# An LSTM cell issued by halves of its units, with the weight sums of a fast product made sooner and in even shares

## The chip, the cores and the metric

The kernel runs on one core of a Trainium2 chip. The metric is device time in microseconds (us) of one execution. A core has TensorE (PE; its weight loads are listed as PEld), VectorE (DVE), ScalarE (ACT), GpSimd (POOL) and SyncE (SP), which run their own instruction streams and wait for one another through semaphores. Here SP only issues DMA transfers, and ACT issues some as well.

## The reference

An LSTM with a residual connection, in fp32. The batch is 32, there are T = 512 steps, and the inputs and the state have 512 elements.

```python
a = x[:, t] @ Wx + b + h @ Wh          # 32 x 2048: gates i, f, o, g
i, f, o = sigmoid(a[:, :512]), sigmoid(a[:, 512:1024]), sigmoid(a[:, 1024:1536])
g = tanh(a[:, 1536:])
c = f * c + i * g                      # c starts at 0, h at cond_1024
h = o * tanh(c)
out[:, t] = x[:, t] + h
```

The product h @ Wh depends on the step before. The product x @ Wx does not, and can be computed ahead.

## The kernel before

**Layout.** The 2048 gate columns of a step are held as a bank of 128 partitions by 512 columns: partition = column group j (four of them) times 32 batch rows, and the 512 columns are two halves of the units, each of which holds i, f, o, g of 64 units. PE works in four column groups of 32, one for each j, so that four matmuls with 32 columns of stationary data run side by side. The profile records each fp32 matmul as two instructions.

**One step.** h_part(t) (L211) adds h @ Wh into the bank: 16 matmuls, for k = 0 to 3 and in each for j = 0 to 3; the stationary operand is the transposed h, `state["ht"][:, k]`. k = 0 and 1 come from the first half of the units, k = 2 and 3 from the second. cell(t) then runs on ACT and DVE: sigmoid of i and f (L225), tanh of g (L226), sigmoid of o (L227) on ACT; f·c for both halves at once (L228), i·g for each half (L230), their sum for each half (L232) on DVE; tanh of c on ACT for each half (L234); h = o·tanh(c) for each half (L236), and two transposes in blocks of 32x32 (L242) on DVE that give the next ht. POOL adds the residual (L247) and SP stores it. From step SPLIT = 478 on, a bank pair is used and the whole cell runs once for each half.

**The products ahead.** The first HEAD = 24 steps use plain products: plain_block (L159), 32 matmuls for each step. Those of steps 0 to 4 go to banks of their own before the first h_part. Those of steps 5 to 23 are emitted two to a step between the h_parts of the head, into one of three banks; keep() (L718) adds the bias on DVE into a parking place in SBUF, and SP stores that into DRAM (kept, L719) and loads it back (L571) when its step is near. Then come 20 groups of 24 steps, whose x @ Wx is made by a scheme with fewer multiplications: each group has 20 slots with seven products of four matmuls (L480, the stream). Its left operands are sums of x (ubuf, made by DVE at L391; the pair sums at L438 and on belong to a loaded group), its right operands are sums of Wx (vdram in DRAM, loaded row by row into vring at L559). The products are evacuated by ACT and DVE (L526 to L542) into cbuf, summed there by DVE (L356), stored to DRAM and loaded into xw some steps later. About 23.3 such matmuls are emitted between two h_parts. Before h_part(t+1) ACT copies xw into the gate bank (seed_step, L588), from step 5 on.

**The weight sums.** tail_sums are eight DVE operations on the loaded Wx; v_slot(s), for 20 slots, makes up to three sums of three DVE operations (L630), which go into vring and ubuf while these are not yet in use, and queues a store of two or three DMAs. flush_v, called after the cell, issues the queued stores from ACT (L642).

**The order of the work** is written out by hand: each engine runs what is emitted for it in program order. In the head each step does, in order: h_part; SP's stores and loads; then for each chunk of PE work the matmuls, and behind the first chunk's matmuls the cell and flush_v, and then keep; then DVE jobs (tail sums, v_slots, four pair sums, early_seeds) from one list, as long as an allowance of 3000 ns of estimated cost for that plain block is left (a v_slot counts 2100); last the seed copy for the next step. When five jobs or fewer are left, the first rows of vring are loaded (load_v_ahead), and when none is left the second group is loaded.

Of the kernel before, what the change touches and what calls it, by code (L numbers as in the profile page):

```python
# [7 lines left out]
F32 = mybir.dt.float32  # L8
AF = mybir.ActivationFunctionType
# [3 lines left out]
P = 128  # L13
B = 32
T = 512
# [4 lines left out]
H = P // 2  # L20
# [3 lines left out]
HEAD = 24  # L24
# [6 lines left out]
KEPT = 5  # L31
# [38 lines left out]
def cost_dve(cols):  # L70
    return 150 + 1.05 * cols
# [17 lines left out]
def kernel(  # L89
# [10 lines left out]
    nc = tc.nc  # L100
    add, sub = nc.vector.tensor_add, nc.vector.tensor_sub
# [34 lines left out]
    def load_x(c, a=0, b=TC):  # L136
        nc.sync.dma_start(
            out=xnat[:, xslot(c), a:b].rearrange("p t q b -> p (t q b)"), in_=x[c][:, a * P : b * P]
        )
# [33 lines left out]
    state = {}  # L173
    sring = [work.tile([P, 2, 4, H], F32, name=f"s_{i}") for i in range(2)]
    oring = [work.tile([P, 2, H], F32, name=f"o_{i}") for i in range(1)]
    fc = work.tile([P, 2, H], F32, name="fc")
    ig = work.tile([P, 2, H], F32, name="ig")
    tanh_c = work.tile([P, P], F32, name="tanh_c")
    hbuf = work.tile([P, P], F32, name="hbuf")
    htr = [work.tile([P, NJ, B], F32, name=f"ht_{i}") for i in range(2)]  # L180
# [34 lines left out]
    def cell(t):  # L215
        n, tt = divmod(t, TC)
        s, nxt = sring[t % 2], sring[(t + 1) % 2]
        o = oring[0]
        ht = htr[t % 2]
        by_gate = lambda a: a.rearrange("p (h g u) -> p h g u", g=G, u=H)  # L220
        for part in [(0,), (1,)] if is_split(t) else [(0, 1)]:
            i = slice(part[0], part[-1] + 1)
            units = slice(H * part[0], H * (part[-1] + 1))
            g = by_gate(half_of(t, part[0])) if is_split(t) else by_gate(bank_of(t))
            nc.scalar.activation(s[:, i, 0:2], g[:, :, 0:2], AF.Sigmoid)  # L225
            nc.scalar.activation(s[:, i, 2], g[:, :, 3], AF.Tanh)  # L226
            nc.scalar.activation(o[:, i], g[:, :, 2], AF.Sigmoid)  # L227
            nc.vector.tensor_mul(fc[:, i], s[:, i, 1], s[:, i, 3])  # L228
            for u in part:
                nc.vector.tensor_mul(ig[:, u], s[:, u, 0], s[:, u, 2])  # L230
            for u in part:
                add(nxt[:, u, 3], fc[:, u], ig[:, u])  # L232
            for u in part:
                nc.scalar.activation(tanh_c[:, HALVES[u]], nxt[:, u, 3], AF.Tanh)  # L234
            for u in part:
                nc.vector.tensor_mul(hbuf[:, HALVES[u]], o[:, u], tanh_c[:, HALVES[u]])  # L236
            if t == T - 1:
                add(tanh_c[:, units], hbuf[:, units], x_last[:, units])
                nc.sync.dma_start(out=out[n][:, tt * P + units.start : tt * P + units.stop], in_=tanh_c[:, units])
                continue  # L240
            for u in part:
                nc.vector.transpose(ht[:, 2 * u : 2 * u + 2].rearrange("p q b -> p (q b)"), hbuf[:, HALVES[u]])  # L242
        if t == T - 1:
            return
        state["ht"] = ht
        oc = ocr[t // 2 % 2]
        (nc.gpsimd if t < T - 8 else nc.vector).tensor_add(oc[:, tt % 2], x_of(t), ht)  # L247
        if tt % 2 == 1 or t == T - 2:
            m = tt % 2 + 1
            stores.append(  # L250
                lambda: nc.sync.dma_start(
                    out=out[n][:, (tt + 1 - m) * P : (tt + 1) * P],
                    in_=oc[:, 0:m].rearrange("p t q b -> p (t q b)"),
                )
            )
            if t == T - 2:
                stores.pop()()
# [7 lines left out]
    room = {"dve": 0.0}  # L265
# [171 lines left out]
    def load_group(g):  # L437
        nc.sync.dma_start(  # L438
            out=xs[g % 2][:, :, 0:4],
            in_=xg[g].rearrange("p (k s m) -> p k s m", k=6, s=4),  # L440
        )
# [249 lines left out]
    def load_seeds(pairs, queue):  # L691
        for i, j in pairs:
            queue.dma_start(out=seeds[i], in_=bias[j : j + 1].to_broadcast([P, W]))
# [14 lines left out]

    parks = [cbuf[:, 8 + i // 2, i % 2 * 2 : i % 2 * 2 + 2].rearrange("p s c -> p (s c)") for i in range(4)]
    park_banks = [xbank[1], xbank[2], bbank]
    kept_stores = []

    def keep(p):
        n = p - KEPT
        dst = parks[n % 4]
        add(dst, park_banks[n % 3], bias_full)  # L718
        kept_stores.append(lambda: nc.sync.dma_start(out=kept[n], in_=dst))  # L719

    with tc.manual_schedule():
# [18 lines left out]
            )  # L740
        load_x(0, 5, 8)
        load_x(1)
        load_x(2)
        load_seeds(((4, 3), (5, 1)), nc.sync)
        load_group(0)
        for n in range(3):
            for j in range(NJ):
                nc.tensor.matmul(
# [6 lines left out]
        for c in range(4):  # L755
            for t in range(KEPT):
                plain_block(t, c, bank_of(t))
        dve_jobs = []
        dve_jobs += [(cost_dve(1024), f) for f in tail_sums(0, 4)]
        for t in range(KEPT):  # L760
            add(bank_of(t), bank_of(t), bias_full)
        dve_jobs += [(cost_dve(1024), f) for f in tail_sums(4, 8)]
        for s in range(R):
            dve_jobs.append((2100.0, lambda s=s: v_slot(s)))
        dve_jobs += [(cost_dve(768), lambda i=i: pair_sum(0, i)) for i in range(4)]
        dve_jobs.append((1600.0, early_seeds))

        fill = [("plain", p) for p in range(KEPT, HEAD)]
        HEAD_STEPS = STREAM0
# [13 lines left out]
        for t in range(T):  # L783
# [8 lines left out]
                load_x(c)  # L792
            if t == SPLIT - 4:
                load_x(NCHUNK - 1)
            if t + 3 >= KEPT and t + 3 < HEAD + NG * GS and t >= 2:
                if t == 2:
                    pass
                load_xw(t + 3)

            if t < HEAD_STEPS:  # L800
                target = head_work * (t + 1) / HEAD_STEPS
                chunks = []
                while done_work < target - 200 and n_plain < HEAD - KEPT:
                    chunks.append(("plain", KEPT + n_plain))
                    n_plain += 1
                    done_work += PLAIN
                n = int((target - done_work) / PROD * 4 + 0.5) if n_plain == HEAD - KEPT else 0
                if t == HEAD_STEPS - 1 and n:
                    n = R * 7 * 4 - pos[0]
                left = n  # L810
                while left > 0:
                    m = min(left, 24)
                    chunks.append(("stream", m))
                    left -= m
                done_work += n * PROD / 4
                for i, (kind, m) in enumerate(chunks):
                    if kind == "plain":
                        bank = park_banks[(m - KEPT) % 3]
                        room["dve"] = 3000.0
                        for cc in range(4):  # L820
                            plain_block(m, cc, bank)
                        if i == 0:
                            cell(t)
                            flush_v()
                        keep(m)
                        if m == HEAD - 1:
                            plains_done = t
                        while dve_jobs and room["dve"] > 0:
                            cost, f = dve_jobs.pop(0)
                            f()  # L830
                            room["dve"] -= cost
                    else:
                        load_v_ahead()
                        u_ahead(m)
                        room["dve"] = m * PROD / 4 * 1.5
                        evacuate()
                        if late_seeds_due and plains_done < t - 1:
                            late_seeds_due.pop()()
                        if t >= HEAD_STEPS - 3 and dve_jobs:
                            dve_jobs.pop(0)[1]()  # L840
                        u_ahead(m + 24)
                        while wqueue and room["dve"] > 0:
                            w_op()
                        seed_banks(m)
                        emit_matmuls(m)
                        if i == 0:
                            cell(t)
                            flush_v()
                            if t == plains_done + 1:
                                load_seeds(((0, 0), (1, 1), (2, 2)), nc.scalar)  # L850
                if t + 1 >= KEPT:
                    seed_step(t + 1)
                if len(dve_jobs) <= 5 and not v_stores:
                    load_v_ahead()
                if group_loaded == 1 and n_plain == HEAD - KEPT and not dve_jobs:
                    assert not v_stores
                    load_group(1)
                    group_loaded = 2
                    dve_jobs += [(cost_dve(768), lambda i=i: pair_sum(1, i)) for i in range(4)]
                continue  # L860


# [91 lines left out]
```

## Time and profile before

| | |
|---|---|
| median of 3 runs | 3188.89 us (3188.05 to 3189.84) |
| the profiled execution | 3188.77 us |
| its span, first to last instruction | 3186.9 us |
| mean granted TensorE clock | 0.996 |
| busy PE, DVE, ACT, POOL | 3140.8, 2161.1, 1344.6, 233.3 us |
| first recurrent product ends | 30.96 us |
| head: recurrent products of steps 4, 5, 6 and 10 end | 72.39, 91.37, 108.04, 152.27 us |
| 24 steps of the steady part | 144.84 to 145.44 us |

The page of a profile gives the busy time of each engine, groups of instructions by line with the idle time ahead of them and what ended it, and the DMA queues. Other views show the waits of a window, the timeline, and the busy time in chosen stretches with the granted clock. L numbers are lines of the kernel. The same lines stand three higher up in the changed kernel from the end of the cell on (L588 becomes L585, L480 L477), and the cell's own lines move a little.

### The profile page before, as it was taken

The numbers are of one execution on the slowest core, as the hardware profiler recorded it, in microseconds if no ns is written. First come the engines' busy times: TensorE is split into PE (matmuls) and PEld (weight loads), VectorE is DVE, ScalarE is ACT, GpSimd is POOL, SyncE is SP. The second block draws the span as 40 slices with busy tenths as digits, with TensorE's granted clock in tenths as the row PEclk, the third lists the DMA queues.
The fourth block names the chain that finished last, engine by engine and source line by source line (L and its number), as shares of the span: only waits on it lengthen the run. The fifth ranks groups of instructions, "written<-read, shape, count | busy, mean of one in ns | idle before, by whom it ended". The sixth has DMA issues, their size and how long they took to land.

```text
span 3186.9 us, 104607 instructions
## 1 busy us (share of the span) xinstructions
PE 3140.8 (99%) x41944; PEld 2017.6 (63%) x41944; DVE 2161.1 (68%) x6763; ACT 1344.6 (42%) x4525; POOL 233.3 (7%) x508
## 2 busy tenths in 40 slices
PE   9799999999999999999999999999999999999998
PEld 6445666666666666666666666656666666666555
DVE  5477767676676767677666767676776767676644
ACT  0134444444444444444444444444444444444344
POOL 0000000000000000000000000000000000000000
PEclk9999999999999999999999999999999999999999
DMA  8777787777777777777787777777777877777831
GB/s 289 251 266 255 236 263 243 254 242 241 261 243 258 229 251 252 253 247 249 241 255 258 226 262 237 258 241 256 242 246 248 255 258 228 247 246 237 261 96 38
DMA packets 310997, 766.64 MB, mean 241 GB/s; under 512 B 49392, under 2 KB 92144, under 8 KB 310000
## 3 DMA queue, kind: packets, MB, share of 16 engines
q1 hardware_dynamic: 296800, 740.82, 71.7%
q10 hardware_dynamic: 13712, 19.14, 1.7%
q8 instruction: 331, 5.42, 0.7%
q14 instruction: 154, 1.26, 0.1%
HBM read 577.04 MB, written 182.71 MB: 238 GB/s over the span
## 4 chain that ended last, share of the span: by engine, by line
PE 83%; DVE 8%; DMA 4%; ACT 2%; issue 1%; SPq 1%; ACTq 1%; DVEq 0%
PE gbank L211 48%; PE xbank L480 26%; PE bbank L480 5%; DVE cbuf L356 3%; PE xbank L211 2%; PE xbank L159 2%; DVE ubuf L391 1%; DMA xw<-xwd 1%; ACT tanh_c L234 1%; DMA xs<-in_L_cond_Wx_dram 1%; DVE ig L230 1%; ACTq L642 1%; DVE fc L228 1%; DVE cbuf L536 1%; ACT cbuf L535 1%
## 5 line engine op out<-in xcount | busy, mean ns | idle before, releaser
L211 PE MATMUL gbank<-wh_sb,ht 128*32 128x512 f32 (+1 forms) x16288 | 1837.6, 581 | 24.0 <-ACT gbank L588 16.5
L211 PEld LDWEIGHTS gbank<-wh_sb,ht 128*32 128x32 f32 x16288 | 785.5, 110 | 749.7 <-issue 577.1
L480 PE MATMUL xbank<-vring,ubuf 128*32 128x256 f32 x14400 | 1159.6, 379 | 6.8 <-DVE cbuf L536 3.0
L480 PEld LDWEIGHTS xbank<-vring,ubuf 128*32 128x32 f32 x14400 | 790.8, 110 | 234.3 <-issue 124.7
L225 ACT ACTIVATE s<-gbank 128x256 f32<-128x256 f32 (+1 forms) x509 | 191.7, 377 | 1360.1 <-PE gbank L211 1335.5
L228 DVE TENSOR_TENSOR fc<-s 128x128 f32<-128x128 f32 (+1 forms) x546 | 153.1, 280 | 743.7 <-ACT s L225 743.4
L356 DVE TENSOR_TENSOR cbuf<-cbuf 128x1024 f32<-128x1024 f32 x480 | 581.2, 1218 | 3.3
L247 POOL TENSOR_TENSOR oc<-xnat,ht 128x128 f32<-128x128 f32 x504 | 233.1, 462 | 2915.9 <-DVE ht L242 1584.4
L234 ACT ACTIVATE tanh_c<-s 128x64 f32<-128x64 f32 x1024 | 210.5, 249 | 281.9 <-DVE s L232 281.0
L588 ACT COPY gbank<-xw 128x512 f32<-128x512 f32 x473 | 283.9, 600 | 27.8 <-DMA vdram<-cbuf 16.4
L236 DVE TENSOR_TENSOR hbuf<-o,tanh_c 128x64 f32<-128x64 f32 x1024 | 193.4, 225 | 139.9 <-ACT tanh_c L234 139.5
L480 PE MATMUL bbank<-vring,ubuf 128*32 128x256 f32 x2400 | 284.3, 379 | 1.4 <-DVE cbuf L532 1.3
L526 ACT COPY cbuf<-xbank 128x512 f32<-128x512 f32 x400 | 233.1, 583 | 69.3 <-PE xbank L480 68.9
L480 PE MATMUL xbank<-vring,r 128*32 128x256 f32 x2400 | 236.9, 379 | 0.2 <-ACT xbank L510 0.2
L480 PE MATMUL xbank<-vring,xs 128*32 128x256 f32 x2400 | 230.3, 381 | 2.9 <-DMA vring<-vdram 2.9
L536 DVE TENSOR_TENSOR cbuf<-xbank,cbuf 128x256 f32<-128x256 f32 x400 | 163.7, 409 | 70.6 <-ACT cbuf L535 70.4
L242 DVE STREAM_TRANSPOSE ht<-hbuf 128x64 f32<-128x64 f32 x1022 | 194.3, 225 | 9.9 <-DVE hbuf L236 2.1
L232 DVE TENSOR_TENSOR s<-fc,ig 128x64 f32<-128x64 f32 x1024 | 184.8, 220 | 2.3
L230 DVE TENSOR_TENSOR ig<-s 128x64 f32<-128x64 f32 x1024 | 184.0, 219 | 0.0
L480 PEld LDWEIGHTS bbank<-vring,ubuf 128*32 128x32 f32 x2400 | 147.8, 110 | 45.1 <-issue 29.9
L532 DVE TENSOR_TENSOR cbuf<-bbank,cbuf 128x256 f32<-128x256 f32 x400 | 162.0, 405 | 4.5 <-PE bbank L480 4.4
L539 DVE TENSOR_TENSOR cbuf<-xbank,cbuf 128x256 f32<-128x256 f32 x400 | 162.5, 406 | 0.1
(84 smaller groups left out, 1916.1 us busy)
## 6 DMA issues: line engine op xcount, KB each, us to landing
vring<-vdram SPq DMA_DIRECT2D x340, 896.0 KB, 5.9
xwd<-cbuf SPq DMA_DIRECT2D x240, 512.0 KB, 6.5
xw<-xwd SPq DMA_DIRECT2D x1920, 64.0 KB, 3.5
out_dram<-oc SPq DMA_DIRECT2D x255, 128.0 KB, 3.0
xnat<-in_x_dram SPq DMA_DIRECT2D x63, 512.0 KB, 5.4
xs<-in_x_grouped_dram SPq DMA_DIRECT2D x10, 1536.0 KB, 10.6
vring<-vdram SPq DMA_DIRECT2D x20, 768.0 KB, 6.3
r<-in_x_grouped_dram SPq DMA_DIRECT2D x10, 1536.0 KB, 10.4
```

Of the source, the lines that this page charges most:

```text
L211: nc.tensor.matmul(dst[j * B : (j + 1) * B], state["ht"][:, k], m, start=False, stop=True, skip_group_check=True)
L225: nc.scalar.activation(s[:, i, 0:2], g[:, :, 0:2], AF.Sigmoid)
L230: nc.vector.tensor_mul(ig[:, u], s[:, u, 0], s[:, u, 2])
L234: nc.scalar.activation(tanh_c[:, HALVES[u]], nxt[:, u, 3], AF.Tanh)
L236: nc.vector.tensor_mul(hbuf[:, HALVES[u]], o[:, u], tanh_c[:, HALVES[u]])
L242: nc.vector.transpose(ht[:, 2 * u : 2 * u + 2].rearrange("p q b -> p (q b)"), hbuf[:, HALVES[u]])
L247: (nc.gpsimd if t < T - 8 else nc.vector).tensor_add(oc[:, tt % 2], x_of(t), ht)
L356: op(c_of(dst), c_of(src), c_of(bb))
L480: nc.tensor.matmul(dst[q * B : (q + 1) * B], left_of(gr, s, r)[:, q * B : (q + 1) * B], vring[:, row % 3, RIGHT[r]], start=start, stop=Tru ...
L526: nc.scalar.copy(t[:, 0:4:3], xb.rearrange("p (n c) -> p n c", n=2))
L536: add(t[:, 1], xb[:, HW:W], t[:, 1])
L588: nc.scalar.copy(bank_of(t), src)
```

## The change

- In the cell, sigmoid of i and f and tanh of g are issued on ACT once for each half of the units, at every step. On DVE one multiplication for each half makes both i·g and f·c (they lie side by side in the state tile), followed by the sum of that half; the transpose of a half stands directly behind its h.
- The eight tail sums are emitted ahead of the bias additions. The 20 slots are given to steps: three each to steps 0 and 1, two each to steps 2 to 8; the four pair sums and early_seeds go to step 9. Within a step they are divided among its plain blocks. The estimated costs and the allowance no longer decide on them.
- The load of the third chunk of x moves to step 3, and the loads of two seeds and of the first group to step 5, all on SP behind that step's stores.
- keep() has six parking places for four.
- The first rows of vring are loaded from step 9 on, and the second group after the jobs of step 9.

```diff
-            nc.scalar.activation(s[:, i, 0:2], g[:, :, 0:2], AF.Sigmoid)
-            nc.scalar.activation(s[:, i, 2], g[:, :, 3], AF.Tanh)
+            for n_, u in enumerate(part):
+                nc.scalar.activation(s[:, u, 0:2], g[:, n_, 0:2], AF.Sigmoid)
+                nc.scalar.activation(s[:, u, 2], g[:, n_, 3], AF.Tanh)
             nc.scalar.activation(o[:, i], g[:, :, 2], AF.Sigmoid)
-            nc.vector.tensor_mul(fc[:, i], s[:, i, 1], s[:, i, 3])
             for u in part:
-                nc.vector.tensor_mul(ig[:, u], s[:, u, 0], s[:, u, 2])
-            for u in part:
-                add(nxt[:, u, 3], fc[:, u], ig[:, u])
+                nc.vector.tensor_mul(prod[:, u], s[:, u, 0:2], s[:, u, 2:4])
+                add(nxt[:, u, 3], prod[:, u, 0], prod[:, u, 1])
             for u in part:
                 nc.scalar.activation(tanh_c[:, HALVES[u]], nxt[:, u, 3], AF.Tanh)
             for u in part:
                 nc.vector.tensor_mul(hbuf[:, HALVES[u]], o[:, u], tanh_c[:, HALVES[u]])
+                if t < T - 1:
+                    nc.vector.transpose(ht[:, 2 * u : 2 * u + 2].rearrange("p q b -> p (q b)"), hbuf[:, HALVES[u]])
...
-            for u in part:
-                nc.vector.transpose(ht[:, 2 * u : 2 * u + 2].rearrange("p q b -> p (q b)"), hbuf[:, HALVES[u]])
...
-    parks = [cbuf[:, 8 + i // 2, i % 2 * 2 : i % 2 * 2 + 2].rearrange("p s c -> p (s c)") for i in range(4)]
+    parks = [cbuf[:, 8 + i // 2, i % 2 * 2 : i % 2 * 2 + 2].rearrange("p s c -> p (s c)") for i in range(6)]
...
-        dst = parks[n % 4]
+        dst = parks[n % 6]
...
-        load_x(2)
-        load_seeds(((4, 3), (5, 1)), nc.sync)
-        load_group(0)
...
-        dve_jobs = []
-        dve_jobs += [(cost_dve(1024), f) for f in tail_sums(0, 4)]
+        for f in tail_sums(0, 4) + tail_sums(4, 8):
+            f()
         for t in range(KEPT):
             add(bank_of(t), bank_of(t), bias_full)
-        dve_jobs += [(cost_dve(1024), f) for f in tail_sums(4, 8)]
+        jobs = {}
         for s in range(R):
-            dve_jobs.append((2100.0, lambda s=s: v_slot(s)))
-        dve_jobs += [(cost_dve(768), lambda i=i: pair_sum(0, i)) for i in range(4)]
-        dve_jobs.append((1600.0, early_seeds))
+            jobs.setdefault(s // 3 if s < 6 else s // 2 - 1, []).append(lambda s=s: v_slot(s))
+        jobs.setdefault(9, []).extend([lambda i=i: pair_sum(0, i) for i in range(4)] + [early_seeds])
+        dve_jobs = []
...
+            if t == 3:
+                load_x(2)
+            if t == 5:
+                load_seeds(((4, 3), (5, 1)), nc.sync)
+                load_group(0)
...
+                todo = jobs.pop(t, [])
+                plains = sum(k == "plain" for k, _ in chunks)
...
-                        while dve_jobs and room["dve"] > 0:
-                            cost, f = dve_jobs.pop(0)
-                            f()
-                            room["dve"] -= cost
+                        last = i == plains - 1
+                        for _ in range(len(todo) if last else -(-len(todo) // (plains - i))):
+                            todo.pop(0)()
...
-                if len(dve_jobs) <= 5 and not v_stores:
+                if t >= 9 and not v_stores:
                     load_v_ahead()
-                if group_loaded == 1 and n_plain == HEAD - KEPT and not dve_jobs:
+                if group_loaded == 1 and n_plain == HEAD - KEPT and not dve_jobs and not jobs:
```

## The prediction

> **What bounds the kernel now.** I read the page's groups first, then busy time by stretches, the waits of the head, and two cells in the timeline. The groups (instructions by line) say what the time is made of; columns are count, busy us, mean ns, idle time before them:
>
> ```profile
> L211 PE MATMUL gbank<-wh_sb,ht 128*32 128x512 f32 (+1 forms) x16288 | 1837.6, 581 | 24.0 <-ACT gbank L588 16.5
> L356 DVE TENSOR_TENSOR cbuf<-cbuf 128x1024 f32<-128x1024 f32 x480 | 581.2, 1218 | 3.3
> L588 ACT COPY gbank<-xw 128x512 f32<-128x512 f32 x473 | 283.9, 600 | 27.8 <-DMA vdram<-cbuf 16.4
> ```
>
> The recurrent matmuls (L211) waited 24.0 us in all, most of it for ACT's seed copy L588, which itself waited for DMAs of the weight sums. The stretches (length, busy us of PE, PEld, DVE, ACT, POOL, then granted clock, DMA share, GB/s) say where:
>
> ```profile
> 72.40:82.70 10.30, 6.90 (x128) 5.36 (x120) 8.25 (x20) 1.12 (x5) 0.46 (x1) 1.00 1.04 371
> 82.70:91.40 8.70, 5.42 (x36) 1.51 (x40) 3.40 (x6) 0.59 (x1) 0.00 (x0) 0.61 0.80 270
> 91.40:99.80 8.40, 3.50 (x64) 2.42 (x56) 6.37 (x16) 1.12 (x5) 0.46 (x1) 1.00 0.75 268
> 99.80:108.10 8.30, 5.84 (x37) 1.56 (x41) 0.00 (x0) 0.59 (x1) 0.00 (x0) 0.59 0.73 252
> 261.50:1185.00 923.50, 922.73 (x12039) 603.24 (x12031) 642.48 (x2018) 405.68 (x1338) 70.31 (x153) 1.00 0.77 249
> ```
>
> From 261.5 us on PE has work all the time (922.73 of 923.50). In the head it has holes, and behind each hole the granted clock is about 0.6. The waits between 60 and 200 us (engine, line, waited for; total us, times, longest):
>
> ```profile
> PE gbank L211 <- ACT gbank L588: 16.5, 3, 7.4
> ACT gbank L588 <- DMA vdram<-cbuf: 16.4, 2, 9.3
> ACT gbank L588 <- DMA vdram<-ubuf: 8.6, 1, 8.6
> ```
>
> So three recurrent products, those of steps 5, 6 and 8, stood still because ACT was issuing stores of weight sums (8, 9, 9, 8, 4 and 8 DMAs in steps 2 to 7) ahead of their seed copy. A full step of the head is 3.43 us of recurrent matmuls and two plain blocks of 3.45, so 10.33; the trace's ends of these products are 72.39 (step 4), 91.37, 108.04, 118.46, 131.52, 141.93 and 152.27 (step 10).
>
> A cell of the steady part, from the end of its matmuls at 1215.90 (start us, length us, instruction):
>
> ```profile
> 1215.97 0.39 ACT L225 ACTIVATE s<-gbank 128x256 f32<-128x256 f32 x1 [2.66 <-PE gbank L211]
> 1216.25 0.27 ACT L226 ACTIVATE s<-gbank 128x128 f32<-128x128 f32 x1
> 1216.38 0.29 DVE L228 TENSOR_TENSOR fc<-s 128x128 f32<-128x128 f32 x1 [0.97 <-ACT s L225]
> 1216.59 0.36 DVE L230 TENSOR_TENSOR ig<-s 128x64 f32<-128x64 f32 x2
> 1217.18 0.40 ACT L234 ACTIVATE tanh_c<-s 128x64 f32<-128x64 f32 x2 [0.49 <-DVE s L232]
> 1217.80 0.37 DVE L242 STREAM_TRANSPOSE ht<-hbuf 128x64 f32<-128x64 f32 x2
> ```
>
> The first transpose ends at +2.136, and the first recurrent matmul could start at +2.285. The recurrent product takes 3.599 by the same trace if it is counted from its first matmul, so the cell alone would allow a step of 5.884; the steady steps are 6.02. Each of the four 32-column groups of PE has 8 recurrent records of 0.4295 and, in a group with six stream matmuls, 12 of 0.216: 6.03. Three of four groups have six in a step of 23. PE, not the cell, sets most steps.
>
> **The cell, worked out.** PE's order is the same in both programs. The costs of 64-column pieces are read from the last 34 steps, where the cell already runs by halves: sigmoid of 128 columns 277 ns, next ACT operation 174 ns after its start; tanh 219, the next one 103 after; dependent DVE operations start about 35 ns after what they wait for, tanh_c 90 after its sum. From the end of the matmuls (ns): sigmoid half 0 at 64, tanh half 0 238 to 457, sigmoid half 1 341, tanh half 1 515 to 734, o 618 to 904. DVE: product of half 0 (128 columns, 291) 490 to 782, sum 817 to 1038, product of half 1 952 to 1243 (it starts 135 behind the sum, as unheld 64-column operations do now), sum 1278 to 1499. tanh_c 1129 to 1386 and 1593 to 1850; hbuf 1417 and 1874; transposes 1748 to 1993 and 2133 to 2378. Before: 1891 to 2136 and 2060 to 2263. **The first half gains 143 ns, the second loses 115.** The third k of the product is the first to need the second half, 1.71 us after its start, so the loss is covered.
>
> What it brings: a step whose three fuller groups fill PE gains nothing. Only every sixth step collects a lead, and in the trace one step of 24 is shorter (5.934 for 6.02): −0.14 there. Three of 24 have the DVE late, with steps of 6.21, 6.08 and 6.21. One, from its matmuls' end at 1185.6:
>
> ```profile
> 1181.90 0.39 ACT L535 COPY cbuf<-xbank 128x256 f32<-128x256 f32 x1
> ...
> 1182.32 0.42 DVE L536 TENSOR_TENSOR cbuf<-xbank,cbuf 128x256 f32<-128x256 f32 x1 [0.47 <-ACT cbuf L535]
> ...
> 1182.99 1.08 DVE L391 TENSOR_TENSOR ubuf<-r 128x896 f32<-128x896 f32 x1
> 1183.98 2.48 DVE L356 TENSOR_TENSOR cbuf<-cbuf 128x1024 f32<-128x1024 f32 x2
> 1186.38 0.29 DVE L228 TENSOR_TENSOR fc<-s 128x128 f32<-128x128 f32 x1
> ```
>
> ACT's copies start behind the second tanh_c, which ends 165 to 170 ns later than now (1850 for 1679), so this DVE chain starts that much later, and the shorter first half pays it back: about +0.02 each. 0.14 − 0.06 = 0.08 per 24 steps, by 19 such periods: **−1.5 us**. Bounds: −19 if the late steps' excess (0.19 + 0.06 + 0.19) goes and four more leads of 0.14 are collected, 1.0 by 19; +19 if the 0.165 falls on six steps of 24 without the payback. I stay near the row-by-row sum. In the split steps at the end (34 of 4.51 us) the second half's transpose comes 30 to 50 ns sooner: **−1**, bounds 0 and −2. The 12.6 us of step 477 (a late weight load) don't change.
>
> The Trainium skill, "VectorE: DVE Perf Modes", section "The DRAIN you can't avoid", says that the next operation waits until the pipe is empty and a semaphore adds nothing; by that, 8 DVE operations for 9 would make the second half earlier, not later. The rows are against it: unheld 64-column operations start 135 ns apart with 220 ns of length, and a dependent one pays 35 more. With the page's rule the second half would gain some 100 ns, which the steady sum would not show.
>
> **The head, worked out.** The start doesn't move: recurrent product 0 ends at 30.96 behind the last weight load (landed 29.85, in a queue served in order, ahead of what is moved), and the eight tail sums of 1.22 us are over before the last plain products (bias additions from 21.97). The stores, spread, are 8, 6, 5, 5, 4, 4, 4, 4 and 6 DMAs in steps 1 to 9. Issues took 0.37, 0.5 and then 0.9 to 1.5 each, so four cost about 2.9 us and eight some 9; step 1's eight hold up nobody, since the first seed copy comes at the end of step 4. Ready times for PE: step 5 starts 79.3 and ends 82.7 (seed copy done about 78.9: close). Then one plain block to 86.15. Here DVE is late: behind the second keep of step 4 (79.35 to 80.05) stands a slot of three sums of three operations each, 2.05 us per sum as between 77.15 and 79.20: to 86.2 (the matmuls of step 5 end at 82.7). Cell of step 5: second tanh_c at about 87.3, four issues 2.9, seed copy 0.6: product 6 starts at 90.85, a **hole of 4.7 us**. Twice a hole of 6.7 to 7.4 us was followed by a clock of 0.6 and a product of 5.44 and 5.78 us for 3.43; I add 2.7, so product 6 ends at 97.0 (now 108.04). Steps 7 to 10 have four stores and DVE time to spare: ends 107.3, 117.7, 128.0 (+0.3 for step 9's six stores), 138.6 against 152.27: **−13.6**. Steps 10 to 11 now take 18.0 us, with waits on seed loads, the second group's load and the ring's third row; those loads are tied to the stores of step 9 and come no sooner, and u sums are 0.65 later: +0.7 to +1.5. Net −12.5. Bounds: −21 without hole and clock, −5 if the hole is as long as now and the end of the head gives some back.
>
> The moved loads land in time: x chunk 2 (0.5 MB, 5.4 us in the median) is issued at 62 and used at about 90, the group (1.5 MB, 10.5) at 83 and used behind 128. Six parks for four only make DVE wait less for kept stores (19 stores of 0.26 MB); I count nothing, since PE does not wait for a park in the rows above; without that cover a keep would wait 2.8 us.
>
> The Trainium skill, "TensorE: Matmul & The Clock Gate", Part 1, has the gate as a free-running window of about 3.4 us that halves the clock after an idle window. Half clock stood for 6.83 us from 82.73 and from 99.79, which agrees; a hole of 4.7 then may or may not hold a whole window, and by the rule the 2.7 us are paid or not, according to where it lies.
>
> **Sum.** 3188.77 (profiled; span 3186.9, and 0.1 from the median 3188.89) − 12.5 − 1.5 − 1 = **3173.7 us**.
>
> **Rivals.** (a) *No hole at step 6* (DVE gets the slot done earlier, clock stays): head −21 to −24, 3163. For: DVE was idle 5.8 us at that point before; against: the nine operations stand in DVE's own order. 12%. (b) *The steady part gains too*: −8 to −19 more, 3160. For: late steps exist; against: the copies that start them move later. 10%. (c) *Slower*: the second half's 115 to 165 ns make ACT's copies and so DVE late in more steps of the 24. Phases 8, 20 and 21 have DVE end 0.2 to 0.56 us after the matmuls now; with the three late ones six steps by 0.165 by 19 are +19. It outweighs the head from 0.66 us per period on. With a head of −8: about 3199. 9%. (d) *The change doesn't do what it says in the head*: the hole at step 6 is as long as now and the loads before step 11 take the rest: −3 to −8, 3184. 14%. Forecast, 3168 to 3180: 55%.
>
> **Numbers.** Range 3161 to 3187: it takes in (a) and the better part of (d), and leaves out (c) and the far end of (b). About 0.2%, 6.4 us, is what a measurement can tell from no change: faster means below 3182.4. Of (d) 0.03 lies beyond it and 0.11 within 0.2%; of (c) 0.01 is within, 0.08 slower; 0.02 of the forecast's case falls short. So faster 0.53 + 0.22 + 0.03 = 0.78, same 0.14, slower 0.08.
>
> **What would show it.** Product ends of 82.7, 97.0 and 138.6 for steps 5, 6 and 10; one wait of some 4.7 us of the recurrent matmuls on the seed copy where there are three; one stretch of 0.6 clock before 140 us where there are two; first transposes ending near +1.99 and second near +2.38; periods of 24 steps within 0.2 us of 144.85. Wrong if steps 5 to 9 stall on stores again, if periods change by over 0.5 us, or if step 10 to 11 grows by over 2.

## The result, and the profile after

The changed kernel takes 3174.11 us in the median of five runs (3171.88 to 3177.82), the kernel before 3188.05 in runs beside it. The ratio is 0.9959, with a 95% interval of 0.9944 to 0.9973. The profiled execution took 3174.11 us, its span is 3172.0, 14.9 us less than the span before. The forecast was 3173.7.

The 14.9 us can be cut up by the ends of the recurrent products (us, before and after):

| stretch | before | after | difference |
|---|---|---|---|
| start to the end of product 0 | 30.96 | 29.93 | −1.03 |
| to product 5 | 60.41 | 51.77 | −8.63 |
| to product 6 | 16.67 | 14.95 | −1.72 |
| to product 9 | 33.89 | 31.10 | −2.79 |
| to product 10 | 10.34 | 11.16 | +0.82 |
| to product 11 | 17.99 | 21.39 | +3.39 |
| to product 20 | 91.27 | 91.69 | +0.42 |
| to the long step ahead of the split | 2748.64 | 2746.01 | −2.63 |
| that step, with the late weight load | 12.59 | 10.36 | −2.23 |
| to the last recurrent product | 159.79 | 159.25 | −0.54 |

Where the holes were, in the same columns as before (length, busy us of PE, PEld, DVE, ACT, POOL, clock, DMA share, GB/s), now cut at the changed kernel's own steps:

```profile
72.40:81.70 9.30, 9.30 (x148) 6.39 (x142) 7.29 (x15) 1.10 (x3) 0.46 (x1) 1.00 0.81 280
81.70:91.40 9.70, 4.79 (x73) 2.91 (x68) 5.69 (x15) 1.95 (x8) 0.46 (x1) 0.89 0.99 352
91.40:99.80 8.40, 8.40 (x91) 3.77 (x85) 1.68 (x8) 1.36 (x7) 0.45 (x1) 0.72 0.48 182
99.80:128.00 28.20, 28.20 (x435) 19.49 (x431) 15.77 (x34) 4.64 (x18) 0.92 (x2) 1.00 0.79 278
139.00:160.30 21.30, 13.30 (x156) 5.57 (x152) 9.21 (x21) 5.10 (x15) 0.45 (x1) 0.76 0.82 297
```

PE is full up to product 5 and from product 6 to 9. One hole of 4.91 us stands in the second row, and the clock falls behind it (0.72 in the third). A new stretch is worse than before: from product 10 to 11 PE is busy for 13.30 of 21.30 us. The waits of PE between 60 and 200 us (total, times, longest) name both:

```profile
PE gbank L210 <- ACT gbank L585: 5.5, 2, 4.9
PE xbank L477 <- DVE cbuf L533: 5.2, 2, 4.4
PE xbank L477 <- DMA vring<-vdram: 3.3, 1, 3.3
```

The first line stood at 16.5 us in three waits. A cell of the steady part, whose matmuls end at 1350.92 (start us, length us):

```profile
1350.97 0.28 ACT L225 ACTIVATE s<-gbank 128x128 f32<-128x128 f32 x1 [2.48 <-PE gbank L210]
1351.15 0.22 ACT L226 ACTIVATE s<-gbank 128x64 f32<-128x64 f32 x1
...
1351.40 0.29 DVE L229 TENSOR_TENSOR prod<-s 128x128 f32<-128x128 f32 x1 [0.80 <-ACT s L226]
...
1351.72 0.23 DVE L230 TENSOR_TENSOR s<-prod 128x64 f32<-128x64 f32 x1
1351.87 0.28 DVE L229 TENSOR_TENSOR prod<-s 128x128 f32<-128x128 f32 x1
...
1352.66 0.25 DVE L236 STREAM_TRANSPOSE ht<-hbuf 128x64 f32<-128x64 f32 x1
...
1353.05 0.24 DVE L236 STREAM_TRANSPOSE ht<-hbuf 128x64 f32<-128x64 f32 x1
```

The transposes end at +1.991 and +2.379; the prediction had 1.993 and 2.378. A period of 24 steady steps is 144.82 us in the median of 18 (145.03 before), and its shortest 144.79 for 144.84. The medians depend on the step at which the periods are cut (other cuts give 0.08 to 0.23 us of difference), so the experiments go by the sum of 18 periods from product 28 on.

### The profile page after: what moved, and what is told of

Read it like the earlier page. It is cut to its first block, busy times and chain, and to the rows that moved or that the text cites. A ratio compares the mean times of both kernels' runs of the same rounds, so it can differ in the third digit from the quotient of the medians.

```text
span 3172.0 us, 105017 instructions
## 1 busy us (share of the span) xinstructions
PE 3127.2 (99%) x41944; PEld 1999.5 (63%) x41944; DVE 2230.0 (70%) x6217; ACT 1453.0 (46%) x5481; POOL 232.9 (7%) x508
## 5 line engine op out<-in xcount | busy, mean ns | idle before, releaser
L210 PE MATMUL gbank<-wh_sb,ht 128*32 128x512 f32 (+1 forms) x16288 | 1885.6, 580 | 20.1 <-ACT gbank L585 5.5
L210 PEld LDWEIGHTS gbank<-wh_sb,ht 128*32 128x32 f32 x16288 | 843.4, 110 | 684.0 <-issue 311.1
L477 PE MATMUL xbank<-vring,ubuf 128*32 128x256 f32 x14400 | 1209.5, 379 | 8.7 <-DVE cbuf L533 5.2
L477 PEld LDWEIGHTS xbank<-vring,ubuf 128*32 128x32 f32 x14400 | 734.7, 110 | 261.9 <-issue 35.8
L225 ACT ACTIVATE s<-gbank 128x128 f32<-128x128 f32 x984 | 276.3, 281 | 1307.9 <-PE gbank L210 1283.7
L229 DVE TENSOR_TENSOR prod<-s 128x128 f32<-128x128 f32 x1024 | 293.2, 286 | 679.0 <-ACT s L226 677.3
L353 DVE TENSOR_TENSOR cbuf<-cbuf 128x1024 f32<-128x1024 f32 x480 | 580.6, 1217 | 3.3
L232 ACT ACTIVATE tanh_c<-s 128x64 f32<-128x64 f32 x1024 | 262.2, 256 | 264.3 <-DVE s L230 260.4
L236 DVE STREAM_TRANSPOSE ht<-hbuf 128x64 f32<-128x64 f32 x1022 | 250.9, 245 | 75.9 <-DVE hbuf L234 2.8
L230 DVE TENSOR_TENSOR s<-prod 128x64 f32<-128x64 f32 x1024 | 230.3, 225 | 35.2
L226 ACT ACTIVATE s<-gbank 128x64 f32<-128x64 f32 x984 | 228.2, 232 | 0.0
```

The costliest lines, as they stand in the source:

```text
L210: nc.tensor.matmul(dst[j * B : (j + 1) * B], state["ht"][:, k], m, start=False, stop=True, skip_group_check=True)
L225: nc.scalar.activation(s[:, u, 0:2], g[:, n_, 0:2], AF.Sigmoid)
L226: nc.scalar.activation(s[:, u, 2], g[:, n_, 3], AF.Tanh)
L229: nc.vector.tensor_mul(prod[:, u], s[:, u, 0:2], s[:, u, 2:4])
L230: add(nxt[:, u, 3], prod[:, u, 0], prod[:, u, 1])
L353: op(c_of(dst), c_of(src), c_of(bb))
```

## The experiments

Times are medians of runs beside the kernel before; the ratio is to that kernel. "Product" means the recurrent product of a step, and in the head a step's time runs from the end of its product to the end of the next. The long step ahead of the split and the start vary between executions (product 0 ends at 29.4 to 31.5 us in thirteen of the fourteen traces and at 33.2 in e10, without relation to an edit), so that a head is compared from product 0 on. Even so, three traces with the very same head (the changed kernel, e9 and e11) have product 10 at 107.4 to 109.0 and product 20 at 222.0 to 223.4 us behind product 0: a difference of 1.5 us in one trace says nothing of an edit.

**The two halves of the change: e1_cell_only and e2_head_only.** e1 is the kernel before with the cell (and its tile `prod`) of the changed one; e2 is the changed kernel with the old cell (`fc`, `ig`). Each is one side of the diff shown above:

```diff
 e1, on the kernel before
-    fc = work.tile([P, 2, H], F32, name="fc")
-    ig = work.tile([P, 2, H], F32, name="ig")
+    prod = work.tile([P, 2, 2, H], F32, name="prod")
...
-            nc.vector.tensor_mul(fc[:, i], s[:, i, 1], s[:, i, 3])
+                nc.vector.tensor_mul(prod[:, u], s[:, u, 0:2], s[:, u, 2:4])
...
 e2, on the changed kernel: the same lines the other way round
```

> The kernel before with the changed cell alone. Theory (the gain is the head's): the head's product ends stay within 1 us of before (91.4 for step 5, 152.3 for step 10), periods of 24 steady steps are 0.05 to 0.15 us shorter, the split steps some 0.4 us in all: 3184 to 3188 us against 3188. Rival (the cell carries a good part of the gain): periods shorter by 0.4 us or more, 3180 or less. Rival (the longer second half costs): periods longer, above 3190.

> The changed kernel with the cell of before: schedule of weight sums, loads and parks alone. Theory: step 5 ends at 81.7 to 82.7, step 6 at 96.7 to 97.2 behind one wait of about 4.7 us, step 10 at 138.5 to 139.5; periods as before (144.84 to 145.4); 3175 to 3179 us. Rival (cell and schedule work together): step 6 or step 10 ends over 1.5 us later than in the changed kernel, 3182 or more.

e1: 3186.09 us, ratio 0.9995 (0.9986 to 1.0004). Products 5 and 10 end at 90.38 and 152.03, so the head is the old one. The interval takes in 1, so the time alone can't tell this gain from none. The periods can: 18 of them together take 2607.3 us for 2610.2 before, 0.16 us each, a little above the expectation. All eight traces with the new cell and the steady allowance unchanged (the changed kernel, e1, e3 to e8) lie at 2606.9 to 2608.0, both with the old cell (before, e2) at 2610.2 and 2610.4. e2: 3179.51 us, ratio 0.9967 (0.9955 to 0.998). Products 5, 6 and 10 end at 82.63, 97.38 and 140.42 behind one wait of 4.7; the 18 periods take 2610.4. The median lies 0.5 us above what was expected. The product of the two ratios is 0.9962, for 0.9959 of both together: within the intervals the parts add, and the schedule carries most of the gain. Neither part alone shortens the long step ahead of the split (12.75 us in e1 and 13.15 in e2), so its −2.23 in the result can't be given to either; with both it took 10.7 to 12.0 us in e3 to e8, and why is not shown. Before, its recurrent product took 5.34 us at half clock, after, 3.64.

**What makes the hole before product 6: e3_sums_regrouped.**

```diff
-            jobs.setdefault(s // 3 if s < 6 else s // 2 - 1, []).append(lambda s=s: v_slot(s))
+            jobs.setdefault(s // 3 if s < 6 else 6 if s == 10 else s // 2 - 1, []).append(lambda s=s: v_slot(s))
```

> The changed kernel; the slot with three sums in a row (slot 11) stands alone behind the first keep of step 4, slot 10 moves to step 6. Theory (the hole before product 6 is DVE's nine operations ahead of cell 5): DVE is free at about 82.8 instead of 85 to 86, the hole falls from 4.9 us to 1 or less, product 6 takes 3.4 to 3.7 us at full clock and ends at 89 to 90 instead of 96.7; everything behind is 6 to 7 us sooner: 3167 to 3168.5. Rival (ACT's stores make the hole): the wait stays above 3 us, 3172 to 3175.

The hole is gone: product 6 ends 6.89 us behind product 5 at full clock, for 14.95. But the edit takes away two things, as slot 10 also brings two of the four stores ahead of the seed copy. In the changed kernel, where product 5 ends at 81.70 (DVE, and ACT's issues):

```profile
83.94 1.28 DVE L627 TENSOR_TENSOR vring<-cbuf,ubuf 128x768 f32<-128x768 f32 x2
85.14 0.28 DVE L229 TENSOR_TENSOR prod<-s 128x128 f32<-128x128 f32 x1
...
86.19 3.19 ACTq L639 DMA_DIRECT2D vdram<-vring  x4
```

In e3, where it ends at 82.92:

```profile
83.51 0.28 DVE L229 TENSOR_TENSOR prod<-s 128x128 f32<-128x128 f32 x1
...
84.55 0.93 ACTq L639 DMA_DIRECT2D vdram<-ubuf  x2
```

DVE starts the cell 3.44 us behind the product in the one and 0.59 in the other, and the stores take 3.19 and 0.93 us to issue. So the late DVE is worth some 2.9 us of the hole of 4.91 and the two stores some 2.3 (estimates from these rows): by them the two together made it, and taking away one alone would not have closed it.

The time is 3173.68 us, ratio 0.9951 (0.9938 to 0.9963), the same as the changed kernel. In the trace 8.1 us are gained at product 6, and 2.0 are left at product 11: up to product 7 come back 2.9, up to product 8, behind six stores (the slot that was moved), 1.6, and up to product 10 1.3. The first of these:

```profile
89.80:103.10 13.30, 10.59 (x165) 6.46 (x160) 9.18 (x19) 1.95 (x8) 0.46 (x1) 1.00 1.04 394
```

```profile
ACT gbank L585 <- DMA vdram<-vring: 7.2, 1, 7.2
...
PE gbank L210 <- ACT gbank L585: 2.7, 1, 2.7
```

In this stretch the DMA engines are full (share 1.04, 394 GB/s), ACT's stores take 7.2 us to be issued, and product 7 waits 2.7 us for the seed copy. The expectation of 3167 was wrong by all of its gain. ACT's second pair of stores was issued at 97.06 and 98.39, just behind the landing of the group load of step 5 (97.05) and of the xw load behind it (98.36).

**The load in step 5: e5_regrouped_early_load and e6_early_load.** Both have the three moved loads back at the start, e5 on top of e3, e6 on the changed kernel:

```diff
         load_x(1)
+        load_x(2)
+        load_seeds(((4, 3), (5, 1)), nc.sync)
+        load_group(0)
...
-            if t == 3:
-                load_x(2)
-            if t == 5:
-                load_seeds(((4, 3), (5, 1)), nc.sync)
-                load_group(0)
```

> The regrouped sums of e3, and in addition the three moved loads (third chunk of x, two seeds, first group) back at the start. Theory (e3 lost its gain again because ACT's stores of step 6 waited for completion semaphores and queue space behind the 1.5 MB group load issued in step 5): the wait of product 7 falls from 2.7 us to under 1, step 6 takes 10.3 to 11 us instead of 13.3, step 10 ends 4 to 6 us sooner than in the changed kernel, 3168 to 3170 us. Rival (the stores are slow by themselves): step 6 takes 12.5 or more, 3172 to 3175.

> The changed kernel with the three moved loads back at the start. Theory (in the changed kernel the load is hidden in the hole before product 6 and the start doesn't depend on it): product ends within 1 us of the changed kernel up to step 10, 3172 to 3176 us. Rival (moving the loads is what made the start 1 us sooner, or what lets the stores pass): product 0 ends at 31 again, or the waits in steps 1 to 6 grow, 3177 or more.

In e5 step 6 takes 10.39 us instead of 13.32, and product 10 stands 103.3 us behind product 0, for 109.0 in the changed kernel: 5.7 sooner, as the theory had it. Its time, 3171.62 us (ratio 0.9952, 0.9939 to 0.9964), is 1.6 above the upper end expected: product 8 now waits 1.8 us behind the six stores of step 7, and product 11 comes 22.3 us behind product 10. e6 has product 10 at 109.8 behind product 0, +0.8, and 3176.37 us (ratio 0.9962, 0.995 to 0.9975), 0.4 above the span expected. So up to product 10 moving the loads made no difference that stands out of the spread of one head: the load in step 5 lay in the hole before product 6, and only without that hole did it cost anything. Behind that nothing can be told: product 20 comes 3.9 us later in e6, but 1.3 later in e11, whose head is the changed kernel's own, and the intervals of the totals overlap.

**The new stretch behind step 9: e4_group_late.**

```diff
-                if group_loaded == 1 and n_plain == HEAD - KEPT and not dve_jobs and not jobs:
+                if t >= 12 and group_loaded == 1 and n_plain == HEAD - KEPT and not dve_jobs and not jobs:
```

> The changed kernel; the second group is loaded at the end of step 12 instead of step 9. Theory (the 21.4 us from product 10 to product 11 come from that load: ACT's third seed load waits for it, and the ring's third row lands behind it): ACT is blocked under 2 us in step 10, the row lands 5 us sooner, step 10 takes 11 to 15 us: 3166 to 3169. Rival (the ring's rows are late on their own, or the first seeds): the wait on the row stays at 3 us and the clock drops anyway, step 10 takes 17 us or more, 3170 or later. A second rival: the load disturbs the rows of steps 12 to 14 and gives back half.

3166.89 us, ratio 0.9928 (0.9915 to 0.9942). Step 10 takes 12.99 us for 21.39, and the clock holds:

```profile
139.20:152.20 13.00, 10.31 (x156) 4.99 (x152) 6.85 (x18) 5.07 (x15) 0.45 (x1) 1.00 0.90 318
```

PE waits 2.7 us in it and nothing for a row of vring. In the changed kernel ACT stood 4.4 us in the three seed loads of step 10, for 1.4 in e4; the third was issued at 146.86, right behind the landing of the second group (146.84), and ACT's copies that free the banks came behind it. The ring's third row landed at 153.25 in the same queue, in e4 at 148.16. Both go with the load, so the theory stands. The three steps behind it are 1.5 us longer together, so the second rival holds for a fifth of the gain at most.

**The parks: e7_four_parks.**

```diff
-    parks = [... for i in range(6)]
+    parks = [... for i in range(4)]
-        dst = parks[n % 6]
+        dst = parks[n % 4]
```

> The changed kernel with four parking places as before. Theory (PE never waits for a park, only DVE could): product ends within 1 us of the changed kernel up to step 10, 3171 to 3178 us, the spread of its own runs. Rival (the two more parks carry some of the gain: a keep on DVE waits for a store and makes the next cell late): some step of 5 to 10 ends over 1.5 us later, 3179 or more.

3176.48 us, ratio 0.996 (0.9945 to 0.9975); product 10 stands 108.8 us behind product 0, for 109.0. The two more parks are worth nothing that can be seen here.

**Why the shorter cell brings so little: e9_even_sums, e10_before_even_sums and e11_sums_off_lead.** In the changed kernel the steps 5.79, 6.24, 6.10 and 6.24 us are the four of a period that can collect PE's lead (where PE's own work leaves room and the cell sets the length). Before, they were 5.93, 6.21, 6.08 and 6.21. e9 (changed kernel), e10 (kernel before) and e11 (changed kernel) shift the sums:

```diff
 e9 and e10
-            room["dve"] = 3800.0 + min(0.0, room["dve"])
+            room["dve"] = 3300.0 + min(0.0, room["dve"])
 e11
-            room["dve"] = 3800.0 + min(0.0, room["dve"])
+            room["dve"] = (3300.0 if t % 6 == 5 else 3800.0) + min(0.0, room["dve"])
```

> The changed kernel with the allowance of DVE time for a steady step 3300 ns instead of 3800, which spreads the sums: at most 3.2 us of them between two cells instead of 3.8. Theory (three of four steps that could collect PE's lead are spoilt by late sums, at 6.24, 6.10 and 6.24 us instead of 5.79): all four come to about 5.8, a period of 24 steps to 143.5 to 143.8 instead of 144.8, 3150 to 3155 us. Rival (another limit, PE's full groups, holds the steps at 6.02): the period falls to 144.2 to 144.4 only, 3163 to 3166. Second rival (sums that come later stop the stream): periods of 144.8 or more.

> The kernel before, old cell and old head, with the allowance of 3300 ns. Theory (each of four leads is worth 6.02 less 5.93 with the old cell, and the halves' 0.14 us count once for each): periods of 144.1 to 144.3, 3173 to 3177 us; so the cell by halves is worth four times 0.14 us a period, some 10 us, once the sums are even, for 1.5 to 2 as it stands. Rival (the sums hold the steps, not the cell): the same period as the changed cell gets with even sums, within 0.15.

e9 took 3260.6 us (ratio 1.0227, 1.0208 to 1.0245), e10 3279.88 (1.0287, 1.0273 to 1.0301): for e9 the second rival, by far, and for e10 neither theory nor rival. Three of four steps with a lead did become about 5.8 us in e9 (5.81, 5.83, 5.85), but one step in each period takes 9.5 to 14.5. In the trace of e9 between 1590 and 1604 us:

```profile
ACT cbuf L523 <- DMA xwd<-cbuf: 6.4, 1, 6.4
...
PE xbank L477 <- ACT xbank L507: 2.2, 1, 2.2
```

ACT's evacuation waited 6.4 us for a buffer of cbuf whose store was not over, and PE stood behind it; the clock of that step was 0.85. Against the changed kernel, e9 runs 221 of its 481 sums (L353) two steps later and 156 one step later. That the store was late because its sums had been put off is the reading that e11 was made to test. e10 has the same waits (38.0 us of PE on ACT's seed copy of the stream over the steady part), so it does not tell what the old cell would make of even sums.

> The changed kernel; the allowance of DVE time is 3300 ns in the steps that can collect PE's lead (every sixth) and 3800 elsewhere, so that a sum is put off by one step at most. Theory (late sums spoil three of four leads; in e9 the ring stalled only because sums were put off by up to three): the three steps of 6.24, 6.10 and 6.24 us come to 5.8 to 5.9, others lose 0.3 at most together, no step above 6.5, a period of 24 steps 143.6 to 144.2 for 144.8: 3152 to 3163 us. Rival (any sum put off stalls the stream): a step of over 7 us a period, 3180 or more.

3160.2 us, ratio 0.9911 (0.9896 to 0.9925). A period takes 143.96 us in the median of 18 for 144.82, no steady step is above 6.5, and the steps with a lead are 5.85, 6.00, 5.95 and 5.83, with 5.95 to 5.99 in the step before each. 74 of the 482 sums run one step later, none later than that. The cause is seen on DVE, ahead of one of these cells. The changed kernel, whose matmuls end at 1465.73:

```profile
1462.62 0.42 DVE L533 TENSOR_TENSOR cbuf<-xbank,cbuf 128x256 f32<-128x256 f32 x1 [0.51 <-ACT cbuf L532]
1462.96 0.41 DVE L536 TENSOR_TENSOR cbuf<-xbank,cbuf 128x256 f32<-128x256 f32 x1
1463.29 1.08 DVE L388 TENSOR_TENSOR ubuf<-r 128x896 f32<-128x896 f32 x1
1464.29 2.48 DVE L353 TENSOR_TENSOR cbuf<-cbuf 128x1024 f32<-128x1024 f32 x2
1466.68 0.28 DVE L229 TENSOR_TENSOR prod<-s 128x128 f32<-128x128 f32 x1
```

The product starts 0.95 us behind the matmuls' end. In e11 one of the two sums (L353) stands in the next step, and the product starts 0.49 us behind their end at 1459.72:

```profile
1457.28 1.08 DVE L388 TENSOR_TENSOR ubuf<-r 128x896 f32<-128x896 f32 x1
1458.28 1.22 DVE L353 TENSOR_TENSOR cbuf<-cbuf 128x1024 f32<-128x1024 f32 x1
1460.21 0.29 DVE L229 TENSOR_TENSOR prod<-s 128x128 f32<-128x128 f32 x1 [0.71 <-ACT s L226]
```

**The head made even: e8_head_even, and both: e12_both.** e8 is e4 and e6 with a list of slots by steps; e12 adds the line of e11.

```diff
-        for s in range(R):
-            jobs.setdefault(s // 3 if s < 6 else s // 2 - 1, []).append(lambda s=s: v_slot(s))
+        plan = ((0, 18, 1), (2, 19, 3), (17, 6, 9), (4, 5), (11,), (7, 12), (8, 10), (13, 14), (15, 16))
+        for when, some in enumerate(plan):
+            jobs[when] = [lambda s=s: v_slot(s) for s in some]
```

> The changed kernel with a list of slots by steps written out: the slots that only store and the two with nine operations in steps 0 to 2, from which no seed copy follows, then two stores to four a step; the moved loads back at the start; the second group's load at the end of step 12. Theory (the head's holes are stores and sums ahead of a seed copy, and the load behind step 9): no hole above 0.5 us from step 4 to step 10, step 5 ends at 82.7, step 6 at 89.6, step 10 at 131 to 132, step 11 at 143 to 146: 3158 to 3162 us. Rival (the head is held by the stores' throughput, whatever their order): step 10 ends at 134 or later, 3164 or more.

> The head of e8 and the steady allowance of e11 together, with the changed cell. Theory (the two places are apart, so their gains add): step 10 ends at 131 to 132, step 11 at 145 to 147, periods of 143.8 to 144.3, the sum 14 to 15 us less for each: 3143 to 3149 us. Rival (the shorter head meets the steady part at another phase of the ring, or the second group's late load disturbs it): periods above 144.5, 3152 or more.

e8: 3159.45 us, ratio 0.9906 (0.989 to 0.9923). PE has no hole from step 4 to product 10, which ends at 131.52:

```profile
72.90:131.50 58.60, 58.60 (x898) 40.36 (x888) 37.51 (x88) 12.29 (x49) 2.75 (x6) 1.00 0.81 283
131.50:146.50 15.00, 12.07 (x157) 5.65 (x160) 9.22 (x22) 5.17 (x15) 0.45 (x1) 0.89 0.93 325
```

The stores' throughput is no limit, then: 283 GB/s carry all of it beside a full PE. Product 11 comes at 146.49, half a microsecond behind the expected span, at a clock of 0.89: the hole in that step was 2.31 us, and half clock followed. e12: 3148.46 us, ratio 0.9876 (0.986 to 0.9893), the fastest of the kernels here; product 10 ends at 129.44 and most periods take 143.8 to 144.5 us. Product 12 came 13.8 us behind product 11 in it, where e8 takes 9.6. DVE's work on the seeds had waited for ACT's third seed load (landed at 143.02) and stood ahead of the cell, which started on DVE 3.4 us behind the end of product 11 (0.9 in e8); PE stood 2.2 us and half clock followed.

## Why the prediction was right

The total was met within 0.4 us, but that is better than its terms, and partly luck: what was missing in the head was made up by a start and a step ahead of the split that no edit explains. Point by point:

- **The bound.** Right: three holes before products 5, 6 and 8 made by ACT's stores. With the stores spread, the wait of products on the seed copy fell from 16.5 to 5.5 us.
- **Products 5, 6 and 10.** Predicted 82.7, 97.0 and 138.6; they ended at 81.70, 96.66 and 138.92. About 1.0 of each is the earlier start, which no edit explains; counted from product 0, they came 0.0, 0.7 and 1.4 us later than worked out.
- **The hole at step 6.** Predicted 4.7 us from nine DVE operations with four issues behind them, measured 4.91; e3 takes away the operations' delay and two of the issues, and the hole goes. The product behind it is listed with 6.59 us, for 3.6 at full clock; 2.7 more were put in.
- **Step 9's six stores.** Put at 0.3, measured 0.82, and 0.0 and 0.7 in the same head in e9 and e11.
- **Steps 10 to 11.** The mis-sized term: +0.7 to +1.5 predicted, +3.39 measured. The working had the group's load behind step 9's stores and the ring's third row behind that, but not that ACT's third seed load would wait for the same load, with ACT's copies behind it: PE stood 4.4 us there and 3.3 on the row. e4 shows it by taking the load away: −8.4 us in this step. In e9 and e11, with the same head, the step took 22.2 and 22.6 us for the 21.39 here, so the term was missed by more, if anything.
- **The head in sum.** −12.5 predicted. To product 20 it was −9.5, of which the start is 1.0. The 3 us too few were made up by the long step ahead of the split (−2.2, put at nothing), which by e1 and e2 belongs to neither part of the change alone, and by the steady part.
- **The cell.** The ends of both transposes to within 5 ns. Per period 0.08 was worked out; the shortest period shortened by 0.05, and 18 periods together by 2.3 us in the changed kernel and 2.9 in e1, for −1.5: the term was too small. Leads moved from 5.93 to 5.79 as worked out, late steps from 6.21 to 6.24. The rest lies in late steps (above 6.05 us) off the regular three of a period: 15 and 17 of them before and in e2, 5 to 8 in the eight traces with the new cell. What makes those was not settled. The prediction set the rows of 64-column operations against the Trainium skill, "VectorE: DVE Perf Modes", section "The DRAIN you can't avoid"; that section goes on to say that a next operation which is not held starts earlier, so the rows were not against it, and the second transposes ended where the rows had them.
- **Rivals.** (a) is what e8 shows can be had (product 10 at 100.0 behind product 0, 21.3 sooner than before), and in the changed kernel did not happen. (b) did not happen, and e11 shows why: the late sums. (c) did not happen, since no further step became late. (d) happened in one place, steps 10 to 11.
- **The parks, the moved loads and the tail sums** were put at nothing. e7 and e6 bear that out for the first two up to product 10, within 0.8 us and so within the spread of one head; the tail sums were not tried alone.
- **The rule of the clock gate.** A hole of 4.91 us here, of 6.7 and 7.4 before, was followed by half clock; holes of 2.7 (e3) and 1.8 us (e5) were not. But one of 2.31 us in e8 was, and one of 3.53 us there, ahead of the split, was not. The Trainium skill, "TensorE: Matmul & The Clock Gate", Part 1, has a free-running window of some 3.4 us, and half clock after an idle one. The window agrees with these traces. If an idle window means one without any work, that part does not: the last section has what they show.

What stays open: how much the shorter cell is worth once the sums are off the steps with a lead. Four times 0.14 us a period, 10 us in all, would be the estimate from 5.93 and 5.79; the old cell was not run with the allowance of e11.

## What to carry to other kernels

A hole is closed for good only if what stands next in line is looked up too: e3 took a hole of 4.9 us away and its time stayed the same, because a load that had lain in it now met the stores of the next step, and the slot that was moved brought a hole of its own. Work that blocks an in-order queue (DMA issues ahead of a copy that PE needs, sums ahead of a cell) belongs where nobody waits behind it, and no further: putting the sums off by one step was worth 14 us, by up to two it cost 86. A shorter chain pays only in the steps that it bounds; look which steps those are and what else stands in them before sizing its gain.

## What the runs showed of the hardware that was not expected

- A DMA issue by ACT can stand still for a transfer of another queue: in the changed kernel ACT's third seed load (0.25 MB) was issued 3.7 us behind the second, right behind the landing of SP's group load of 1.5 MB, and in e3 two stores by ACT were issued within 0.1 us of the landing of SP's loads. In the trace these issues carry the completion semaphore of the load that had just landed.
- Half clock goes by stretches of a fixed grid, not by the length of a hole alone. In each of the fourteen traces the changes of the granted clock lie whole multiples of 3.41 us apart. Cut by that grid, from 20 us after the start to 12 us before the end, 62 stretches at full clock had 2.09 us or more without a PE matmul, and all 62 were followed by half clock; of 27 with 1.91 to 2.02 us four were, and of those with less none. e8's hole of 2.31 us (136.72 to 139.03) lies whole in the stretch that ends at 139.33; its hole of 3.53 us (2984.44 to 2987.97) is cut into 1.6 and 1.9. By these figures a hole of 4.2 us or more is always followed by half clock (an estimate: 2.1 of it lie in one stretch wherever it begins), and a shorter one by where it lies.
- So traces differ in whole products: the product ahead of the split took 5.26 to 5.34 us in five of the fourteen and 3.64 in nine, by the clock granted at that place, which gave or took 1.7 us of a total.
